# Gathered rows copied by ScalarE before TensorE weights them, one round later

## The chip, the cores and the metric

The kernel runs on one core of one Trainium2 chip. The metric is the device time of one execution in microseconds. Before the change it is 7,739.45 us, the median of three runs (7,736.22 to 7,743.75).

## The reference, cut to what matters

Four layers follow each other on a tensor of 4 images, 256 channels, 64 x 64 pixels; each adds its result to its input. The change is in layer 0, a deformable convolution. For every pixel, each of 4 groups of 64 channels and each of 9 points, an offset is computed from the image, and the padded image is read at that place between four neighbouring pixels. The four readings are weighted by the position and by a softmax mask, and the nine points are added up:

```python
return tap(x0, y0, (1 - wx) * (1 - wy)) + tap(x0 + 1, y0, wx * (1 - wy)) + tap(x0, y0 + 1, (1 - wx) * wy) + tap(x0 + 1, y0 + 1, wx * wy)
...
samp = _grid_sample(img, sg)
mr = mask.reshape(n, H * W, G, P).transpose(0, 2, 1, 3).reshape(n * G, 1, H * W, P)
dout = (samp * mr).sum(-1).reshape(n, G * GC, H * W).transpose(0, 2, 1).reshape(n, H, W, C)
dout = jnp.einsum('nhwc,oc->nhwo', dout, outproj_w) + outproj_b
```

The places depend on the data, so the readings are gathers. The rest of layer 0 (convolutions, a squeeze-and-excite and two large matrix products called the feed-forward), layer 1 (linear attention with a 5 x 5 depthwise convolution), layer 2 (a 3 x 3 convolution) and layer 3 (attention against a pooled map) are dense work.

## The kernel before, in words

Each image has a table in HBM (`tab`) in which one row holds the 2 x 2 neighbourhood of a pixel for one group: 256 values of fp32, 1 KB. `sample(n, ssum)`, lines 556 to 686, does the gathering of image n in rounds. A round is 14 pixels by 9 points, 126 of the 128 partitions, and all four groups. An image has 4,096 pixels, so it has 293 rounds in 19 blocks of up to 16; four images have 1,172 rounds.

What happens to round i, and on which engine:

- `gathered`, lines 596 to 608: GpSimd issues four indirect DMAs, one a group (line 600), each of 128 rows of 1 KB, into a tile `g` of 4 KB a partition. There are seven such tiles (`bufs=7`), so the first DMA of round i waits until TensorE has read the tile of round i - 7. The four DMAs also use eight landing semaphores in turn, so each waits until the DMA eight before it has landed.
- Still in `gathered`, line 607: TensorE multiplies the four landed pieces with a small weight matrix `wm`, 8 matmuls of 128 columns, which the trace records as 16. They add up into one half of a PSUM bank, `acc`; two rounds make a unit.
- `weigh`, line 591: VectorE makes `wm` for four rounds at once, four rounds ahead, into one of two buffers.
- `moved`, line 612: ScalarE copies the unit's sums to SBUF (`at`). `turned`, line 617: TensorE transposes them. `spread`, line 632: ScalarE puts them in their places (`dT`). `project`, `add`, `finish` (lines 640, 644, 649): a matmul, an addition and a scaling at the end of each block.

**What sets the order.** The order on TensorE, VectorE, ScalarE and GpSimd is the order in which the program issues instructions: `ordered()`, line 1217, switches the scheduler's own reordering off for these four. Each engine works through its own queue and stops at the first instruction whose semaphores are not there yet. Two things decide what stands where in the queues:

- The dictionary `later` in `sample`. Step i of the loop first runs what has been put down for step i, then issues the gathers of round i. Before the change, `moved`, `turned` and `spread` of a unit that ends in round i run at steps i + 1, i + 2 and i + 3 (the last one step later in the first rounds of a block).
- `beside`, line 1194. After each step it lets other generators advance in proportion: beside image 0 the convolutions and offsets of images 1 to 3; beside image n the feed-forward of image n - 1 during the first fifth of the rounds and its layer 1 (`linear`) after that, and beside images 2 and 3 also layers 2 and 3 of image n - 2. Their instructions stand between the steps of `sample` in the same queues. This document calls them the side work.

GpSimd's queue holds nothing but gathers while images are sampled. After the last gather, dense work of images 2 and 3 remains.

Of the kernel before, what the change touches and what calls it, by code (L numbers as in the profile page):

```python
# [9 lines left out]
F32 = mybir.dt.float32  # L10
# [7 lines left out]
P = 128  # L18
N, C, H, W = 4, 256, 64, 64
HW = H * W  # L20
KT = C // P
NB = HW // 512
NT = HW // P
G, PT = 4, 9
# [5 lines left out]
RP, WR, UR, BR = 14, 4, 2, 16  # L30
# [41 lines left out]
class Net:  # L72
# [483 lines left out]
    def sample(self, n, ssum):  # L556

        nc, sp = self.nc, self.sp
        table = self.tab[n].rearrange("g y x s c -> (g y x) (s c)")
        blocks, images, at, dp, dT, po, later = {}, {}, {}, {}, {}, {}, {}

        def halves(name):

            t = self.ps1.tile([P, 2, 256], F32, name=name, tag=name)
            return cycle([t[:, 0], t[:, 1]])

        accs, dps = halves("acc"), halves("dp")  # L570

        def load(b):
            p0, np_ = BLOCKS[b]
            whole, part = np_ // RP, np_ % RP

            nr = whole + (part > 0)
            sl = sp.tile([P, BR, G * 5], F32, name="sl")
            rows = self.s_d[n][p0 * PT:p0 * PT + nr * RS, :].rearrange("(r p) f -> p r f", p=RS)
            more = self.s_d[n][p0 * PT + RS:p0 * PT + (nr + 1) * RS, :].rearrange("(r p) f -> p r f", p=RS)
            nc.sync.dma_start(sl[0:RS, 0:nr], rows)  # L580
            nc.sync.dma_start(sl[RS:P, 0:nr], more[0:P - RS])
            rounds = [(r, RP) for r in range(whole)] + [(whole, part)] * (part > 0)
            blocks[b] = sl, rounds

        def weigh(b, r):

            sl, rounds = blocks[b]
            nu = min(WR, len(rounds) - r)
            wm = self.gp.tile([P, WR, 4 * G, OB], F32, name="wm")
            sh = [P, nu, 4 * G, OB]  # L590
            nc.vector.tensor_tensor(  # L591
                wm[:, 0:nu], self.con("own").unsqueeze(1).unsqueeze(1).to_broadcast(sh),
                sl[:, r:r + nu, G:].unsqueeze(3).to_broadcast(sh), ALU.mult)
            return wm

        def gathered(sl, wm, acc, r):
            r4, acc = r % WR, acc[:, r % UR * P:(r % UR + 1) * P]
            g = self.gp.tile([P, G, 256], F32, name="g", bufs=7)
            for i in range(G):
                nc.gpsimd.indirect_dma_start(  # L600
                    out=g[:, i, :], out_offset=None, in_=table,
                    in_offset=bass.IndirectOffsetOnAxis(ap=sl.bitcast(I32)[:, r, i:i + 1], axis=0))


            for x in range(2):
                for i in range(G):
                    nc.tensor.matmul(acc[32 * i:32 * i + 32, :], wm[:, r4, 4 * i + 2 * x:4 * i + 2 * x + 2, :],  # L607
                                     g[:, i, x * P:(x + 1) * P], start=x == 0, stop=x == 1)

        def moved(acc, nu, u):  # L610
            at[u] = sp.tile([P, UR, P], F32, name="at")
            nc.scalar.copy(at[u].rearrange("p v c -> p (v c)")[:, 0:nu * P], acc[:, 0:nu * P])  # L612

        def turned(nu, u):
            dp[u] = next(dps).rearrange("p (v g s o) -> p v g s o", v=UR, g=G, s=2)
            for v in range(nu):
                nc.tensor.transpose(dp[u][:, v].rearrange("p g s o -> p (g s o)"), at[u][:, v], self.ident)  # L617

        def spread(unit, b, u):

            if b not in dT:
                p0, np_ = BLOCKS[b]
                dT[b] = sp.tile([P, G, BP], F32, name="dT", bufs=1)
                images[b] = sp.tile([P, KT, BP], F32, name="yb")
                nc.sync.dma_start(images[b][:, :, 0:np_], self.y_d[n][:, :, p0:p0 + np_])
            full = sum(1 for _, m in unit if m == RP)
            for v0, v1, m in ((0, full, RP), (full, len(unit), unit[-1][1])):
                for s in range(2):
                    if v0 < v1:
                        hs = slice(64 * s, 64 * s + 64)  # L630
                        q0 = RP * (unit[0][0] + v0)
                        nc.scalar.copy(  # L632
                            dT[b][hs, :, q0:q0 + m * (v1 - v0)].rearrange("p g (v o) -> p g v o", o=m),
                            dp[u][hs, v0:v1, :, s, 0:m].rearrange("p v g o -> p g v o"))

        def project(b, m):
            np_ = BLOCKS[b][1]
            po[m] = self.ps("po")
            for k in range(G):
                nc.tensor.matmul(po[m][:, 0:np_], self.ow[:, k, m * P:(m + 1) * P], dT[b][:, k, 0:np_], start=k == 0, stop=k == G - 1)  # L640

        def add(b, m):
            ym = images[b][:, m, 0:BLOCKS[b][1]]
            nc.vector.tensor_tensor(ym, po[m][:, 0:BLOCKS[b][1]], ym, ALU.add)

        def finish(b, m):
            p0, np_ = BLOCKS[b]
            ym = images[b][:, m, 0:np_]
            nc.scalar.activation(ym, ym, AF.Identity, bias=self.sh[:, 4 + m:5 + m],
                                 scale=self.inv[:, 4 + m:5 + m], accum_out=ssum[:, m, b:b + 1])  # L650
            if m == KT - 1:
                nc.sync.dma_start(self.x2_d[n][:, :, p0:p0 + np_], images[b][:, :, 0:np_])

        load(0)
        order = [(b, r) for b, (_, np_) in enumerate(BLOCKS) for r in range(-(-np_ // RP))]
        wm = weigh(0, 0)
        for i, (b, r) in enumerate(order):
            for f in later.pop(i, ()):
                f()
            sl, rounds = blocks[b]  # L660
            if r % UR == 0:
                acc = next(accs)
            gathered(sl, wm, acc, r)
            if r == 0 and b + 1 < len(BLOCKS):
                load(b + 1)
            ends = r + 1 == len(rounds)
            if r % WR == 0:
                if r + WR < len(rounds):
                    nxt = weigh(b, r + WR)
                elif b + 1 < len(BLOCKS):  # L670
                    nxt = weigh(b + 1, 0)
            if r % UR == UR - 1 or ends:
                unit = rounds[r - r % UR:r + 1]
                todo = [partial(moved, acc, len(unit), i), partial(turned, len(unit), i), partial(spread, unit, b, i)]

                todo = [(i + 1 + j + (j == 2 and r < UR), f) for j, f in enumerate(todo)]
                if ends:
                    todo += [(i + 4 + m + j, partial(f, b, m)) for m in range(KT) for j, f in enumerate((project, add, finish))]
                for j, f in todo:
                    later.setdefault(j, []).append(f)  # L680
            if r % WR == WR - 1 or ends:
                wm = nxt
            yield 1
        for i in sorted(later):
            for f in later[i]:
                f()
# [656 lines left out]
```

## Time and profile before

| what | value |
|---|---|
| median of the timed runs | 7,739.45 us |
| span of the profiled execution (the page gives no other time for it) | 8,805.8 us |
| first and last start of a gather in it | 134.1 and 7,306.6 us |
| busy, TensorE / VectorE / ScalarE / GpSimd | 5,993.9 / 5,173.3 / 2,183.8 / 5,152.4 us |
| mean granted TensorE clock | 0.809 |
| gathers | 4,688 indirect DMAs, 614.77 MB, 225,024 packets |
| share of the DMA engines' time, gathers / other copies | 24.3% / 16.4% |

How to read it. The profiled execution is 1,066.4 us longer than the median of the timed runs, so durations of single instructions can be taken from it, but not all of its waiting. A GpSimd gather counts as busy while GpSimd makes its descriptors; the data lands later. Idle time ahead of an instruction is put down to the work whose semaphore ended it ("releaser"); "remote" stands for a release that the profile can't put down to a recorded end, and "issue" for a gap in which nothing was waited for. The lines of the page that matter are shown with the prediction.

### The profile page before, as it was taken

How to read it: one execution, taken by the hardware profiler on the slowest of the kernel's cores; microseconds unless marked ns; L12 is line 12 of the kernel's file. 1: busy time of each engine (PE TensorE's matmuls, PEld its weight loads, DVE VectorE, ACT ScalarE, POOL GpSimd, SP SyncE). 2: the span in 40 equal slices, each digit the busy share in tenths (PEclk: the TensorE clock that was granted, in tenths of full speed). 3: DMA queues.
4: the chain of work that ended last, by engine and by line, in shares of the span. 5: the costliest groups of instructions: out<-in, count | busy, mean ns of one | idle time of the engine just before them, and what ended most of it. 6: DMA issues, size and time to landing. Idle time of an engine off the chain costs nothing. (4 is left out here: it accounts for less than half of the span.)

```text
span 8805.8 us, 95736 instructions
## 1 busy us (share of the span) xinstructions
PE 5993.9 (68%) x36532; PEld 3575.6 (41%) x36532; DVE 5173.3 (59%) x6409; ACT 2183.8 (25%) x4899; POOL 5152.4 (59%) x4950
## 2 busy tenths in 40 slices
PE   4454554448744446688876677888766778986899
PEld 2222222224323322244544443345544433664477
DVE  5444443443466667424777776227777772599834
ACT  1111111112211112122223222222222222465524
POOL 2666666566666666666666656666666661376410
PEclk7676766669866667799988888898878888998999
DMA  6454454444433334444443344444434343220131
GB/s 172 127 155 124 141 154 118 125 145 145 153 105 105 110 105 129 127 130 138 134 135 110 112 121 136 142 134 132 136 115 117 114 118 99 69 74 29 48 98 53
DMA packets 759050, 1042.27 MB, mean 118 GB/s; under 512 B 362432, under 2 KB 472128, under 8 KB 757056
## 3 DMA queue, kind: packets, MB, share of 16 engines
q0 software_dynamic: 225024, 614.77, 24.3%
q1 hardware_dynamic: 533568, 421.39, 16.4%
q8 instruction: 289, 4.73, 0.2%
q14 instruction: 169, 1.38, 0.0%
HBM read 867.08 MB, written 168.69 MB: 118 GB/s over the span
## 5 line engine op out<-in xcount | busy, mean ns | idle before, releaser
L600 POOL DMA_INDIRECT g<-tab,sl x4688 | 4618.5, 985 | 2687.8 <-issue 1224.2
L178 DVE SCALAR_TENSOR_TENSOR agg<-pad,vec,agg 128x1024 f32<-128x1024 f32 x2280 | 2933.5, 1287 | 61.9
L607 PE MATMUL acc<-g,wm 128*32 128x128 f32 x18752 | 1034.8, 333 | 1907.8 <-ACT at L612 1273.7
L607 PEld LDWEIGHTS acc<-g,wm 128*32 128x32 f32 x18752 | 566.8, 128 | 2411.7 <-ACT at L612 1446.1
L1048 PE MATMUL ps<-xd,w 128*128 128x256 f32 x3072 | 752.7, 396 | 51.3 <-issue 37.8
L591 DVE TENSOR_TENSOR wm<-con,sl 128x1024 f32<-128x1024 f32 (+1 forms) x296 | 357.7, 1209 | 711.9 <-remote 533.5
L1048 PEld LDWEIGHTS ps<-xd,w 128*128 128x128 f32 x3072 | 595.1, 199 | 175.0 <-issue 86.0
L632 ACT COPY dT<-dp 64x112 f32<-64x112 f32 x1176 | 285.9, 243 | 1043.7 <-remote 544.3
L742 PE MATMUL ps<-x2f,f 128*128 128x512 f32 x1024 | 499.2, 636 | 19.1 <-issue 7.7
L817 PE MATMUL ps<-xr,qw 128*128 128x512 f32 x768 | 472.0, 746 | 22.1 <-issue 11.1
L727 DVE SCALAR_TENSOR_TENSOR hm<-ps,vec,lk 128x512 f32<-128x512 f32 x256 | 190.8, 750 | 492.9 <-ACT lk L744 405.5
L752 PE MATMUL ps<-hm,f 128*128 128x512 f32 x1024 | 467.1, 605 | 0.9 <-DVE hm L727 0.9
L612 ACT COPY at<-acc 128x256 f32<-128x256 f32 (+1 forms) x588 | 218.3, 371 | 986.3 <-remote 753.2
L999 POOL TENSOR_TENSOR xd<-xp 128x640 f32<-128x640 f32 x64 | 79.4, 1268 | 492.6 <-ACT xp L1011 298.3
L640 PE MATMUL po<-dT,ow 128*128 128x224 f32 (+1 forms) x1216 | 326.1, 419 | 45.4 <-issue 19.3
L617 PE MATMUL dp<-ident,at 128*128 128x128 f32 x1172 | 284.1, 330 | 106.6 <-ACT dT L632 61.0
L865 ACT COPY kt<-pt 128x512 f32<-128x512 f32 x256 | 149.4, 584 | 829.3 <-remote 403.8
L744 ACT ACTIVATE lk<-ps,low 128x512 f32<-128x512 f32 x256 | 174.0, 687 | 666.0 <-PE ps L742 512.1
L1147 PE MATMUL s<-ph,th 128*128 128x512 f32 x512 | 290.2, 672 | 62.5 <-ACT kt L865 15.9
L640 PEld LDWEIGHTS po<-dT,ow 128*128 128x128 f32 x1216 | 265.5, 233 | 113.8 <-issue 68.9
L1167 PEld LDWEIGHTS ps<-gt,pT 128*128 128x128 f32 x2048 | 276.0, 213 | 70.8 <-issue 46.1
L194 POOL TENSOR_TENSOR ak<-ak,m 128x1024 f32<-128x1024 f32 x96 | 228.1, 2376 | 130.6 <-ACT m L193 126.7
(243 smaller groups left out, 8022.0 us busy)
## 6 DMA issues: line engine op xcount, KB each, us to landing
g<-tab,sl POOLq DMA_INDIRECT x4688
x<-x SPq DMA_DIRECT2D x128, 512.0 KB
xr<-x SPq DMA_DIRECT2D x96, 512.0 KB
tab<-xo SPq DMA_DIRECT2D x192, 128.0 KB
x<-in_x SPq DMA_DIRECT2D x32, 512.0 KB
y<-yc SPq DMA_DIRECT2D x32, 512.0 KB
x2f<-x SPq DMA_DIRECT2D x32, 512.0 KB
xyf<-x SPq DMA_DIRECT2D x32, 512.0 KB
```

What stands on the lines that cost most here:

```text
L178: nc.vector.scalar_tensor_tensor(to, s, wt, acc, ALU.mult, ALU.add)
L591: nc.vector.tensor_tensor(wm[:, 0:nu], self.con("own").unsqueeze(1).unsqueeze(1).to_broadcast(sh), sl[:, r:r + nu, G:].unsqueeze(3).to_bro ...
L600: nc.gpsimd.indirect_dma_start(out=g[:, i, :], out_offset=None, in_=table, in_offset=bass.IndirectOffsetOnAxis(ap=sl.bitcast(I32)[:, r, i: ...
L607: nc.tensor.matmul(acc[32 * i:32 * i + 32, :], wm[:, r4, 4 * i + 2 * x:4 * i + 2 * x + 2, :], g[:, i, x * P:(x + 1) * P], start=x == 0, st ...
L617: nc.tensor.transpose(dp[u][:, v].rearrange("p g s o -> p (g s o)"), at[u][:, v], self.ident)
L632: nc.scalar.copy(dT[b][hs, :, q0:q0 + m * (v1 - v0)].rearrange("p g (v o) -> p g v o", o=m), dp[u][hs, v0:v1, :, s, 0:m].rearrange("p v g ...
L640: nc.tensor.matmul(po[m][:, 0:np_], self.ow[:, k, m * P:(m + 1) * P], dT[b][:, k, 0:np_], start=k == 0, stop=k == G - 1)
L742: nc.tensor.matmul(ps, f1[:, k, m * P:(m + 1) * P], x2[:, k], start=k == 0, stop=k == KT - 1)
L752: nc.tensor.matmul(ps, f2[:, k, m * P:(m + 1) * P], hm[:, k], start=k == 0, stop=k == 4 * KT - 1)
L817: nc.tensor.matmul(ps, qw[:, k, m * P:(m + 1) * P], x[:, k], start=k == 0, stop=k == KT - 1)
L1048: nc.tensor.matmul(ps[:, e], w[:, k, t, 2 * half + e, m * P:(m + 1) * P], v[:, 2 * half + e, k, t:t + 8], start=i % 6 == 0, stop=i % 6 == 5)
L1147: nc.tensor.matmul(s[i], tv[:, 4 * b + j], ph[:, i * 512:(i + 1) * 512], start=True, stop=True)
```

## The change

Round i is split over three steps. At step i GpSimd issues the gathers, now into four tiles `g`. At step i + 1 ScalarE copies the landed tile, 128 partitions by 1,024 values, to one of three tiles `gc`. At step i + 2 TensorE weights the copy. A tile `g` is thus free when ScalarE has copied it, and a tile `gc` when TensorE has read it. The memory is the same: 4 + 3 tiles in place of 7. What follows the weighting moves by two steps (`moved`, `turned`, `spread`), `project`, `add` and `finish` by three, and `weigh` is issued at steps 2, 6, 10 and 14 of a block for the same rounds as before, so still four steps ahead of its use.

```diff
-        def gathered(sl, wm, acc, r):
-            r4, acc = r % WR, acc[:, r % UR * P:(r % UR + 1) * P]
-            g = self.gp.tile([P, G, 256], F32, name="g", bufs=7)
+        def gathered(sl, r):
+            g = self.gp.tile([P, G, 256], F32, name="g", bufs=4)
             for i in range(G):
                 nc.gpsimd.indirect_dma_start(
                     out=g[:, i, :], out_offset=None, in_=table,
                     in_offset=bass.IndirectOffsetOnAxis(ap=sl.bitcast(I32)[:, r, i:i + 1], axis=0))
-
-
+            return g
+
+        def copied(g, i):
+            held[i] = self.gp.tile([P, G, 256], F32, name="gc", bufs=3)
+            nc.scalar.copy(held[i], g)
+
+        def weighted(wm, acc, r, i):
+            r4, acc, g = r % WR, acc[:, r % UR * P:(r % UR + 1) * P], held.pop(i)
             for x in range(2):
                 for i in range(G):
                     nc.tensor.matmul(acc[32 * i:32 * i + 32, :], wm[:, r4, 4 * i + 2 * x:4 * i + 2 * x + 2, :],
...
-            gathered(sl, wm, acc, r)
+            g = gathered(sl, r)
+            for j, f in ((1, partial(copied, g, i)), (2, partial(weighted, wm, acc, r, i))):
+                later.setdefault(i + j, []).append(f)
...
-            if r % WR == 0:
-                if r + WR < len(rounds):
-                    nxt = weigh(b, r + WR)
+            if r % WR == 2:
+                if r + 2 < len(rounds):
+                    nxt = weigh(b, r + 2)
                 elif b + 1 < len(BLOCKS):
                     nxt = weigh(b + 1, 0)
...
-                todo = [(i + 1 + j + (j == 2 and r < UR), f) for j, f in enumerate(todo)]
+                todo = [(i + 3 + j + (j == 2 and r < UR) * (7 - 5), f) for j, f in enumerate(todo)]
                 if ends:
-                    todo += [(i + 4 + m + j, partial(f, b, m)) for m in range(KT) for j, f in enumerate((project, add, finish))]
+                    todo += [(i + 7 + m + j, partial(f, b, m)) for m in range(KT) for j, f in enumerate((project, add, finish))]
```

In the built program the number and the order of GpSimd's gathers are the same as before; the first gather of each round now waits for ScalarE's semaphore where it waited for TensorE's. ScalarE's queue has 1,172 more copies. Within a step the program issues `moved` ahead of the copy, so that in ScalarE's queue each second copy stands right behind an `at` copy, and the side work of the step stands behind both.

More of the change, by code (lines that the diff above doesn't have):

```diff
@@ L562, in sample @@
         table = self.tab[n].rearrange("g y x s c -> (g y x) (s c)")
-        blocks, images, at, dp, dT, po, later = {}, {}, {}, {}, {}, {}, {}
+        blocks, images, at, dp, dT, po, held, later = {}, {}, {}, {}, {}, {}, {}, {}
         def halves(name):
```

## The prediction

> **What bounds the kernel now.** I read the groups of the page first, then who waited on GpSimd, then its timeline, then the busy times by stretch.
>
> ```profile
> L600 POOL DMA_INDIRECT g<-tab,sl x4688 | 4618.5, 985 | 2687.8 <-issue 1224.2
> L607 PE MATMUL acc<-g,wm 128*32 128x128 f32 x18752 | 1034.8, 333 | 1907.8 <-ACT at L612 1273.7
> L612 ACT COPY at<-acc 128x256 f32<-128x256 f32 (+1 forms) x588 | 218.3, 371 | 986.3 <-remote 753.2
> L865 ACT COPY kt<-pt 128x512 f32<-128x512 f32 x256 | 149.4, 584 | 829.3 <-remote 403.8
> ```
>
> ```profile
> POOL g L600 <- issue: 1224.2, 4007, 0.7
> POOL g L600 <- remote: 624.7, 307, 6.0
> POOL g L600 <- PE acc L607: 494.3, 201, 23.2
> ```
>
> ```profile
> 1009.60 0.95 POOL L600 DMA_INDIRECT g<-tab,sl  x1 [0.30 <-issue]
> 1010.85 0.95 POOL L600 DMA_INDIRECT g<-tab,sl  x1 [0.30 <-issue]
> 1013.81 0.94 POOL L600 DMA_INDIRECT g<-tab,sl  x1 [2.02 <-remote]
> ```
>
> A gather takes GpSimd 0.95 us and 0.30 us to the next: 1.25 us, 5.0 us a round. 4,688 x 1.25 = 5,860 us. From the first gather at 134.1 to the end of the last at 7,307.5 us are 7,173 us, so 1,313 us are longer gathers and stops. The stops stand at the first gather of a round, the one that waits for a free tile: GpSimd has used up its seven tiles and TensorE has not read the oldest. "Remote" is the same wait: at 1,013.81 TensorE's recorded matmuls had ended earlier than the release.
>
> ```profile
> 3669.00:4050.00 381.00, 315.54 (x1654) 148.61 (x1644) 93.76 (x132) 82.33 (x193) 240.40 (x249) 0.92 0.46 135
> 4050.00:5487.00 1437.00, 1049.87 (x7011) 669.40 (x7010) 1053.45 (x1241) 371.64 (x916) 903.92 (x924) 0.85 0.44 127
> ```
>
> Columns: stretch, length, busy PE, PEld, DVE, ACT, POOL, clock, DMA. The first stretch is the feed-forward beside image 2: 249 gathers are 62 rounds, 315.5 / 62 = 5.1 us of TensorE a round against GpSimd's 5.0. In the second, 231 rounds, VectorE needs 1,053.5 / 231 = 4.6 us a round. GpSimd bounds, but TensorE, then VectorE, are within 10%. ScalarE is the idle one: 371.6 of 1,437.
>
> The profiled execution is 1,066.4 us longer than the median. If a gather costs the same without the profiler and the rest keeps its length, a timed run has room for only 1,313 - 1,066 = 247 us of stops. GpSimd is then nearly the whole bound of the gathering stretch.
>
> **What the Trainium skill says.** "DMA: Bandwidth & Descriptors", section on the anatomy of one SWDGE DMA: "DMA engines do not wait on semaphores"; the wait is on the issuing sequencer. So one full ring holds all gathers behind it, as the timeline shows. The page gives some 2.0 us from issue to completion; here 225,024 packets / 4,688 are 48 a gather, and in order of time the 48th ends 1.4 to 2.5 us after its issue: it agrees. "GPSIMD Engine Reference", section "When to use GPSIMD": GpSimd's cores generate the descriptors, so the 0.95 us are not shortened by how the data is used later. "ScalarE: Activation LUTs", section "What ACT_TABLE_LOAD costs": 186 ns + 0.833 ns an element with immediate operands. The trace has 372 ns (median) for 256 columns and 584 for 512, a slope of 0.83: it agrees.
>
> **The change, part by part.**
>
> *The copies.* 1,172 copies of 1,024 columns. From the trace, 584 + 2 x 212 = 1,008 ns, read from PSUM; from the page an estimate of 1,039. I take 1.04 us: 1,172 x 1.04 = 1,219 us more ScalarE, 2,184 -> 3,403. Per image ScalarE gets 305 us on top of 248, 340, 454 and 454 (busy by image): at most 759 of 1,821 us. It does not become the bound by load. What it can do is delay the ScalarE link of a chain: `lk` before VectorE's `hm`, `kt`, `pr`, `at`. Such an instruction finds a copy running with chance 1.04 / 6.1 = 17%, and then waits 0.52 us: 0.09 us each. Images 2 and 3 have 1,108 ScalarE instructions in 293 rounds, 3.8 a round; if two of them are waited for, 0.18 us a round. That is paid only where side work is behind GpSimd; I take 40% of the 879 rounds of images 1 to 3: 0.18 x 352 = 65 us. Bounds: 0, if PSUM and tile buffers cover it; 0.34 x 879 = 300 us if all 3.8 count everywhere. The copy also waits, for its landing and for a `gc` tile, and the side work of the step stands behind it. Landing comes 2.5 us after GpSimd's round, the copy a step later, so this wait costs nothing while GpSimd is a round ahead.
>
> *The shorter ring.* The memory stays seven tiles, but they no longer give one distance. Before, GpSimd stops when TensorE has not finished round i - 7: six rounds, 30.0 us, less 2.5 of landing and some 1.0 of matmuls, about 26 us that TensorE may be held. Now it stops when ScalarE has not copied round i - 4: three rounds, 15.0 - 2.5 - 1.04 = 11.5 us that ScalarE may be held. And ScalarE's queue is held by all others: each second copy stands behind `at`, which waits for TensorE. In the gathering stretch ScalarE idled over 11.5 us 63 times; the excess over 11.5 is 81 us in 32 waits with a named releaser (VectorE's `agg`, TensorE's `ps`) and 130 us in 31 "remote" ones, 53 of it in one wait at the start of sampling that comes before any ring is full. Where GpSimd was stopped anyway, nothing is lost. I take three quarters of the named: 60 us. Bounds: 0 and 81 + 77 = 158.
>
> *The later weighting.* TensorE no longer stops for a landing. TensorE waited for landings 9 times, 30.7 us, 21.1 of them at the first round of all, which stays. Gain 0 to 10 us; I take 0, since such a stop comes when GpSimd is the late one. `wm` is still made four steps ahead of its use and waits for the same TensorE step, so VectorE's waits do not move. `acc` is reused at the same distance. No DMA is added or moved past another on GpSimd's queue; on SP's the loads of `sl` and the stores of blocks keep their steps within three.
>
> *The end.* One more copy after the last landing: 1 us. At the ends of images 0 to 2 GpSimd goes on with the next image and covers it.
>
> Sum: 65 + 60 + 0 + 1 = +126 us. Against the profiled execution's own time that is 8,805.8 + 126 = 8,932 us of span; the page gives no time around the span. The work added is the same in a timed run, so I put the same sum on the median: 7,739.45 + 126 = 7,865 us (+1.6%). What is late next, once GpSimd has stopped for a copy, is TensorE or VectorE as before; they get no shorter.
>
> **The rivals.**
>
> *Hidden, 7,739 us.* ScalarE is idle for 60% of every image even with the copies, and the total of seven tiles is kept. For it: the side work's matmuls have three PSUM tiles in turn (`mm`), so a ScalarE delay of 1 us is mostly buffered. Against it: ScalarE's long waits, which the ring must now absorb.
>
> *Faster, 7,640 us.* A tile is freed by ScalarE as soon as it landed, not by TensorE after everything ahead of it in its queue. The place is GpSimd's wait at line 600. Its price: the stops named after TensorE, 494.3 - 201 x 0.30 = 434 us, of which half, the copies that do not stand behind an `at`, could go: 217 us in the profile; a timed run has room for 247 us of stops in all, so about 100 there. It decides where TensorE is late and ScalarE is not, by more than one step: `at` waits for TensorE every second step, so ScalarE can't run away from it. That speaks against it.
>
> *ScalarE sets the pace of side work, 8,105 us.* If each copy stands in a chain TensorE - ScalarE - VectorE, then 879 rounds x 1.04 us x 40% = 366 us. For it: TensorE's greatest wait is already for ScalarE's `at` (1,273.7 us). Against it: those waits end with TensorE's own completion, and ScalarE itself is idle in them.
>
> **How the numbers follow.** Forecast 0.62, its own range 7,800 (the copies cost nothing, +61) to 7,970 (half of both upper bounds, (300 + 158) / 2 = 229). Hidden 0.12. Faster 0.12. ScalarE pacing 0.14. A difference of 0.2%, 15 us, is about what a measurement of this kernel tells from no change. Slower: 0.62 + 0.14 = 0.76; same 0.12; faster 0.12. The range of 7,690 to 8,110 starts halfway between the faster and the hidden case and ends just past the pacing case: it leaves out half of each of the two outer cases, 0.06 + 0.07, and with the forecast's own tails about 0.17.
>
> **What would show it.** Right: GpSimd's waits at the first gather named after ScalarE's `gc` copy and longer in sum than the 1,119 us of before; gathers still 0.95 + 0.30 us; copies of about 1.04 us, ScalarE busy near 3,400 us; TensorE's weighting waiting for almost nothing but `gc`. The ring is the larger cost if the stops grow where ScalarE waits long; the copies, if TensorE's and VectorE's waits for ScalarE's side work grow instead. Wrong: stops well below 1,119 us, or a gather with another duration; also if the sampling ends at the same time and the difference lies in the dense work after it, which the change doesn't touch.

## The result, and the profile after

The changed kernel takes 7,831.5 us (median of 4 runs, 7,825.3 to 7,834.7) against 7,741.6 us for the kernel before (4 runs): a ratio of 1.0111, 95% interval 1.0099 to 1.0123. It is slower by 90 us, where the forecast had 126.

One thing is needed to read the numbers. The profile of before shown ahead of the prediction seems to come from a chip of a second sort. On two such chips the unchanged kernel took 8,820 and 8,755 us in timed runs (experiments 4 and 6), at granted clocks of 0.80 to 0.81; that profile has 8,805.8 us and 0.809. On the other chips the kernel takes 7,740 us, at 0.84 to 0.85. If so, the 1,066 us between that profile and the timed runs come from the chip, and not from the profiler. A second profile of before, on a chip of the first sort, has a span of 7,730.1 us, close to its timed runs, and no "remote" at GpSimd's gathers; it is what the profile after (span 7,823.5 us) is compared with. I call it "before, again".

Groups of before, again, with all releasers the view gives (busy us, mean ns of one | idle before it):

```profile
L600 POOL DMA_INDIRECT g<-tab,sl x4688 | 4593.2, 980 | 1651.7 <-issue 1311.9 <-DMA sl<-sd 135.6 <-PE acc L607 112.2
L607 PE MATMUL acc<-g,wm 128*32 128x128 f32 x18752 | 1328.3, 319 | 1101.5 <-DMA g<-tab,sl 575.5 <-ACT at L612 517.4 <-issue 3.1
L612 ACT COPY at<-acc 128x256 f32<-128x256 f32 (+1 forms) x588 | 218.3, 371 | 625.8 <-PE acc L607 604.4 <-issue 12.8 <-ACT dT L632 0.3
```

The same groups after:

```profile
L599 POOL DMA_INDIRECT g<-tab,sl x4688 | 4584.6, 978 | 1761.1 <-issue 1304.6 <-ACT gc L606 236.0 <-DMA sl<-sd 132.4
L606 ACT COPY gc<-g 128x1024 f32<-128x1024 f32 x1172 | 1218.9, 1045 | 1706.9 <-DMA g<-tab,sl 1706.2 <-ACT ot L922 0.2
L612 PE MATMUL acc<-gc,wm 128*32 128x128 f32 x18752 | 933.7, 328 | 1521.4 <-ACT at L617 1254.4 <-ACT gc L606 266.5
L617 ACT COPY at<-acc 128x256 f32<-128x256 f32 (+1 forms) x588 | 218.2, 371 | 41.0 <-PE acc L612 18.6 <-PE ps L759 10.3
```

A gather costs GpSimd what it did (978 and 980 ns, and the same gaps named "issue"). The waits for landings, 575.5 us, have gone from TensorE and are now ScalarE's, 1,706.2 us: whoever reads the tile first waits for GpSimd, and since GpSimd bounds, that need not cost time (experiment 2). These landings make up 1,706.2 of the 1,706.9 us that ScalarE idled ahead of its copies, so the three tiles `gc` never held it up. What changed on the engine that bounds stands in the first line of each fence: 112.2 us of waits for TensorE became 236.0 us of waits for ScalarE's copy. GpSimd's waits in order of size (us in total, times, longest) show it again, first before, again, then after:

```profile
POOL g L600 <- issue: 1311.9, 4306, 0.6
POOL g L600 <- PE acc L607: 112.2, 88, 7.0
```

```profile
POOL g L599 <- issue: 1304.6, 4282, 0.6
POOL g L599 <- ACT gc L606: 236.0, 129, 21.5
```

From the first gather to the end of the last are 6,109.3 us in before, again, and 6,213.3 after, 104 us more; what follows the last gather is 7 us shorter. So the loss lies in the gathering stretch. There I count **stops**: the gap ahead of a round's first gather where it is over 0.35 us, less the usual 0.30, and without the first of all. They sum to 87 us in before, again, and 197 after. The 110 us more cover the whole loss.

The stretches of image 2, feed-forward first and then layer 1 with layers 2 and 3 of image 0, in before, again (length, busy PE, PEld, DVE, ACT, POOL with the number of instructions, clock, DMA share, GB/s):

```profile
3168.00:3480.00 312.00, 276.81 (x1495) 132.27 (x1494) 85.95 (x119) 73.80 (x170) 235.13 (x244) 0.96 0.53 159
3480.00:4703.00 1223.00, 981.57 (x7148) 636.48 (x7147) 1055.02 (x1253) 380.86 (x938) 910.18 (x930) 0.90 0.51 150
```

and after:

```profile
3201.30:3523.00 321.70, 287.25 (x1546) 136.70 (x1547) 88.07 (x122) 131.79 (x236) 229.30 (x237) 0.96 0.51 151
3523.00:4774.00 1251.00, 995.41 (x7151) 649.66 (x7150) 1054.44 (x1250) 603.99 (x1166) 916.09 (x937) 0.89 0.51 148
```

In the long stretch VectorE does the same work (1,055 and 1,054 us) and GpSimd too, ScalarE has 223 us more and is still busy for less than half of it. The stretch is 28 us longer, of which some 9 are the seven gathers more that fall into it (937 against 930). No engine got full; GpSimd was let go later.

### The profile page after: what moved, and what is told of

Read it like the earlier page. It is cut to its first block, busy times and chain, and to the rows that moved or that the text cites. A ratio compares the mean times of both kernels' runs of the same rounds, so it can differ in the third digit from the quotient of the medians.

```text
span 7823.5 us, 98450 instructions
## 1 busy us (share of the span) xinstructions
PE 5714.5 (73%) x36532; PEld 3477.0 (44%) x36532; DVE 5157.9 (66%) x6409; ACT 3319.8 (42%) x6071; POOL 5118.5 (65%) x4950
## 5 line engine op out<-in xcount | busy, mean ns | idle before, releaser
L612 PE MATMUL acc<-gc,wm 128*32 128x128 f32 x18752 | 933.7, 328 | 1521.4 <-ACT at L617 1254.4
L606 ACT COPY gc<-g 128x1024 f32<-128x1024 f32 x1172 | 1218.9, 1045 | 1706.9 <-DMA g<-tab,sl 1706.2
L612 PEld LDWEIGHTS acc<-gc,wm 128*32 128x32 f32 x18752 | 531.1, 126 | 1973.0 <-ACT at L617 1486.6
L1055 PE MATMUL ps<-xd,w 128*128 128x256 f32 x3072 | 715.1, 386 | 21.4 <-ACT kt L872 15.0
L645 PE MATMUL po<-dT,ow 128*128 128x224 f32 (+1 forms) x1216 | 302.8, 401 | 21.4 <-DVE yb L649 8.8
L1174 PE MATMUL ps<-gt,pT 128*128 128x128 f32 x2048 | 296.9, 306 | 6.7 <-ACT pT L1170 6.6
L1161 ACT ACTIVATE pe<-s,mx 128x512 f32<-128x512 f32 x256 | 173.6, 683 | 302.0 <-DVE mx L1156 302.0
L749 PEld LDWEIGHTS ps<-x2f,f 128*128 128x128 f32 x1024 | 191.4, 195 | 234.1 <-issue 217.0
L194 POOL TENSOR_TENSOR av<-av,m 128x1024 f32<-128x1024 f32 x96 | 226.7, 2362 | 99.8 <-ACT m L193 95.4
```

Source lines behind the costliest of these rows:

```text
L194: nc.gpsimd.tensor_tensor(acc, acc, m, ALU.add)
L606: nc.scalar.copy(held[i], g)
L749: nc.tensor.matmul(ps, f1[:, k, m * P:(m + 1) * P], x2[:, k], start=k == 0, stop=k == KT - 1)
L1055: nc.tensor.matmul(ps[:, e], w[:, k, t, 2 * half + e, m * P:(m + 1) * P], v[:, 2 * half + e, k, t:t + 8], start=i % 6 == 0, stop=i % 6 == 5)
L1174: nc.tensor.matmul(ps[:, 0:P], pT[:, m], gt[:, m], start=m == 0, stop=m == 7)
```

## Where one stop comes from

The longest stop after, in GpSimd's timeline (start, us; in brackets the idle time before it and what ended it):

```profile
1366.51 0.94 POOL L599 DMA_INDIRECT g<-tab,sl  x1 [0.30 <-issue]
1367.76 0.95 POOL L599 DMA_INDIRECT g<-tab,sl  x1 [0.30 <-issue]
1390.16 1.28 POOL L599 DMA_INDIRECT g<-tab,sl  x1 [21.45 <-ACT gc L606]
```

and ScalarE's timeline over the same time:

```profile
1351.26 1.04 ACT L606 COPY gc<-g 128x1024 f32<-128x1024 f32 x1 [4.76 <-DMA g<-tab,sl]
...
1357.29 1.02 ACT L482 ACTIVATE t<-agg 128x1024 f32<-128x1024 f32 x1 [4.32 <-DVE agg L178]
1371.59 1.02 ACT L482 ACTIVATE t<-agg 128x1024 f32<-128x1024 f32 x1 [13.27 <-DVE agg L178]
1387.71 0.44 ACT L537 ACTIVATE ml<-ml 128x288 f32<-128x288 f32 x1 [15.10 <-DVE ml L536]
...
1388.84 1.99 ACT L606 COPY gc<-g 128x1024 f32<-128x1024 f32 x2
```

Between the copy that ended at 1,352.3 and the one that started at 1,388.84 ScalarE copied nothing for 36.5 us. The offsets of a later image stood in its queue, and three of their instructions in a row waited for VectorE: 4.3, 13.3 and 15.1 us. Four tiles let GpSimd issue three rounds past the one that ScalarE owes, about 15.0 us; 36.5 - 15.0 = 21.5 us is the length of the stop. In before, again, the corresponding stop is 7.0 us, although ScalarE is held longer there:

```profile
1394.81 1.04 POOL L600 DMA_INDIRECT g<-tab,sl  x1 [6.96 <-PE acc L607]
```

```profile
1362.41 1.02 ACT L482 ACTIVATE t<-agg 128x1024 f32<-128x1024 f32 x1 [15.34 <-DVE agg L178]
1376.70 1.02 ACT L482 ACTIVATE t<-agg 128x1024 f32<-128x1024 f32 x1 [13.27 <-DVE agg L178]
1392.14 0.44 ACT L537 ACTIVATE ml<-ml 128x288 f32<-128x288 f32 x1 [14.42 <-DVE ml L536]
```

There TensorE, which frees the tiles, waits for ScalarE's `at` behind these three, but seven tiles stand between it and GpSimd.

A wait of ScalarE is only the beginning of a stop. Summed over all 72 stops of after (218.6 us, the usual 0.30 us of each included), ScalarE waited for other engines for 66 us. For 58 us it was copying gathered tiles, for 75 us it did other work, and 19 us lie between the end of a copy and the gather that it lets go. So the stop lasts until ScalarE has worked off what piled up ahead of the copy that is owed.

## Experiments

Each is compared with the kernel before, run beside it on the same chip. The table has the kernels run on chips of the first sort: the time, its ratio, then from the profile the sum of the stops and the time from an image's first gather to the next one's (for image 3, to the end of its last gather).

| kernel | median us | ratio (95%) | stops | image 0 | 1 | 2 | 3 |
|---|---|---|---|---|---|---|---|
| before, again | 7,738.9 | 1.0006 (0.9997 to 1.0014) | 87 | 1,518.2 | 1,514.7 | 1,535.1 | 1,541.3 |
| lag_only | 7,745.4 | 1.0010 (1.0004 to 1.0017) | 108 | 1,526.1 | 1,519.2 | 1,547.0 | 1,544.7 |
| copies_only | 7,788.3 | 1.0064 (1.0050 to 1.0078) | 144 | 1,524.9 | 1,515.2 | 1,565.1 | 1,572.1 |
| ring4 | 7,833.0 | 1.0130 (1.0112 to 1.0147) | 192 | 1,553.7 | 1,528.5 | 1,571.7 | 1,562.1 |
| after | 7,831.5 | 1.0111 (1.0099 to 1.0123) | 197 | 1,549.2 | 1,518.4 | 1,572.6 | 1,573.1 |
| thin4_b | 7,807.1 | 1.0083 (1.0069 to 1.0096) | 167 | 1,548.8 | 1,521.7 | 1,556.0 | 1,556.2 |
| thin7_b | 7,750.7 | 1.0007 (1.0001 to 1.0014) | 100 | 1,517.5 | 1,521.0 | 1,542.2 | 1,545.9 |

My theory at the start of this part: GpSimd bounds, and it pays for the shorter ring and for the copies' time on ScalarE in about equal parts. The rivals: the ring alone; the copies alone; the later weighting.

**1. The kernel before, unchanged** (before_again), to have a profile to compare with.

> The kernel before, unchanged, for a second profile. The profile of the changed kernel has a span of 7,823.5 us, within 8 us of its median, and its GpSimd is rarely stopped; the first profile of before was 1,066 us longer than its median. If that first profile was disturbed, this one has a span near 7,740 us, next to no waits named remote, and stops of GpSimd at the first gather of a round of about 100 us in place of 1,119. If the profiler always stretches this kernel, the span is again near 8,800 us.

Measured 7,738.9 us and the profile used above. The waits named "remote" are absent, so they belong to the first profile's chip and not to the kernel.

**2. The later weighting alone** (lag_only): TensorE weights the gathered tile itself two steps later; seven tiles, no copies.

```diff
+        def copied(g, i):
+            held[i] = g
...
-            gathered(sl, wm, acc, r)
+            g = gathered(sl, r)
+            for j, f in ((1, partial(copied, g, i)), (2, partial(weighted, wm, acc, r, i))):
+                later.setdefault(i + j, []).append(f)
```

(with the other steps of the queue moved as in the change)

> One part alone: TensorE weights two rounds after the gather, as in the changed kernel, but reads the gathered tile itself; seven tiles g, no copies. Ring theory and copy theory: the lag costs nothing of its own; GpSimd now stops when TensorE's step is five rounds behind it where it was seven, so 7,740 to 7,760 us. Rival, that the lag itself costs (later chain at block ends, weights made at another step): 7,790 to 7,830 us. A gain is possible if TensorE's stops for landings mattered: 7,700 us.

Measured +0.1%, some 7 us, as both theories had it. It gains nothing, although TensorE in before, again, waited 575.5 us for landings. Its waits in lag_only:

```profile
PE acc L611 <- DMA g<-tab,sl: 597.1, 706, 21.2
PE acc L611 <- ACT at L616: 526.4, 308, 12.1
```

They are still there: TensorE reaches the weighting early whatever its place in the queue, because GpSimd is the late one.

**3. The copies alone, and the shorter ring alone.** copies_only is the kernel before in which ScalarE also copies 1,024 columns of a constant a round, in three pieces, to a tile that nobody reads; by the profile they take 1.43 us a round (two of 512 ns, one of 405) in place of 1.045, and they wait for no gather. ring4 is the kernel before with four gather tiles.

```diff
+            spare, flat = self.gp.tile([P, 384], F32, name="gc", bufs=1), self.ow.rearrange("p g c -> p (g c)")
+            for a, b in ((0, 384), (384, 768), (768, 1024)):
+                nc.scalar.copy(spare[:, 0:b - a], flat[:, a:b])
```

```diff
-            g = self.gp.tile([P, G, 256], F32, name="g", bufs=7)
+            g = self.gp.tile([P, G, 256], F32, name="g", bufs=4)
```

> The other cost alone: the kernel before with seven tiles, and in each round ScalarE also copies 1,024 constant columns (in three pieces, about 1.2 us) to a spare tile that nothing reads and that wait for nothing but each other. Copy theory: 7,800 to 7,850 us, with VectorE's and TensorE's waits for ScalarE grown. Ring theory: within 25 us of before, since ScalarE has the idle time.

> One cost alone: the kernel before with four gather tiles in place of seven, TensorE reading them in the same step. GpSimd stops when TensorE has not finished the round four before. Ring theory: slower by as much as the change or more, 7,820 to 7,950 us, with stops of GpSimd growing by that amount. Copy theory: the ring has slack to spare, within 15 us of before.

Measured +0.64% (50 us) for the copies and +1.30% (101 us) for the ring. The ring's 7,833 us are where the ring theory had them; the copies' 7,788 us lie above what the ring theory allowed and below what the copy theory had. Each alone is a cost, and with lag_only they make 2.04%, nearly twice the 1.11% of the change: they do not add up. The place differs too. copies_only loses 30 us in each of images 2 and 3 in the profiled execution, which was the slowest of its five. Most of it lies in rounds 240 to 269 (201.2 us against 172.4 in image 2, against 178.7 in image 3), where layers 1 to 3 run beside the gathers. ring4 loses in all four images, 36 us of it in image 0, where one stop alone is 23.3 us (7.0 before):

```profile
POOL g L600 <- PE acc L607: 230.1, 127, 23.3
```

What each part costs inside the changed kernel was still open. The next pair asks that.

**4. The changed kernel with small copies** (thin4), and with seven gather tiles on top (thin7). Small copies free the memory for it. Both leave out most of the gathered values, so what they add up is not the convolution.

```diff
-            held[i] = self.gp.tile([P, G, 256], F32, name="gc", bufs=3)
-            nc.scalar.copy(held[i], g)
+            held[i] = self.gp.tile([P, G, 32], F32, name="gc", bufs=3)
+            nc.scalar.copy(held[i], g[:, :, 0:32])
...
-                                     g[:, i, x * P:(x + 1) * P], start=x == 0, stop=x == 1)
+                                     g.rearrange("p g c -> p (g c)"), start=x == 0, stop=x == 1)
```

> The changed kernel (four gather tiles, three of the copy, weighting two steps later), but ScalarE copies only 32 of each round's 4x256 gathered columns per slot, and all eight matmuls read these 128 columns. It leaves out the other columns, so that its output is not the convolution; gathers, waits and order stay. ScalarE loses some 0.77 us a round (1,045 ns down to about 270 ns, 900 us in sum). If the shorter ring is the cost (a stall that ScalarE or GpSimd inherits from other work costs GpSimd time once four rounds are out), the time stays within 7,800 to 7,830 us, and GpSimd's gathers still wait for the copy some 150 to 240 us. If the time of the copies themselves is the cost, it falls to 7,745 to 7,770. I expect the first, with a part of the second: 7,800.

> As the one before, but with seven gather tiles in place of four (the small copies leave room). Copies, their order and the later weighting stay, so only the length of the ring differs between the two. If the ring is the cost, 7,735 to 7,755 us, as the kernel before, and waits of gathers for the copy under 100 us. If what costs is that GpSimd waits for a queue with more in it (ScalarE, behind at) whatever the ring, it stays over 7,780.

Both ran on a chip on which the kernel before took 8,820.1 us: 9,529.8 us (ratio 1.0785, 1.0758 to 1.0812) and 9,522.3 us (1.0799, 1.0779 to 1.0819). Neither theory had such numbers. On this chip four tiles or seven make no difference with small copies, so the ring is not the cost there. Experiment 6 has more of it.

**5. The same two kernels, on a chip of the first sort.**

> The kernel with copies of 32 columns a slot and four gather tiles once more (it leaves out the other columns), because the call before ran on a chip on which the kernel before takes 8,820 us. On a chip where the kernel before takes 7,740 us: ring theory 7,800 to 7,830 us, copy theory 7,745 to 7,770; I expect 7,800. On a chip such as the last one: 9,530 again.

> The kernel with copies of 32 columns a slot and seven gather tiles once more. On a chip where the kernel before takes 7,740 us: ring theory 7,735 to 7,755 us; if a stop comes whatever the ring, over 7,780. On a chip such as the last one: 9,520 again.

7,807.1 and 7,750.7 us, both as the ring theory had it. Their groups of the copy, and GpSimd's wait for it, thin4_b first:

```profile
L606 ACT COPY gc<-g 128x128 f32<-128x128 f32 x1172 | 343.8, 298 | 2251.6 <-DMA g<-tab,sl 2249.6 <-issue 1.4
```

```profile
POOL g L599 <- ACT gc L606: 195.2, 98, 18.6
```

and thin7_b:

```profile
POOL g L599 <- ACT gc L606: 126.6, 87, 8.9
```

This splits the change in three, in ratios, each to the kernel before that ran beside it. The time of the copies, 1,045 down to 298 ns: 1.0111 - 1.0083 = 0.28%, 22 us. The ring, four tiles to seven: 1.0083 - 1.0007 = 0.76%, 59 us. What is left, the later weighting and the small copies: 0.07%, 5 us. The ring's part rests on two kernels that differ in the number of tiles alone; it is measured with small copies, and with full ones it may differ. The copies' part is barely resolved by the times (one interval starts at 1.0099, the other ends at 1.0096), and the changed kernel and thin4_b were not run side by side. The profiles place it: after loses to thin4_b 16.6 and 16.9 us in images 2 and 3 and nothing in images 0 and 1. The ring's 56 us in the profiles are 31 in image 0, 1 in image 1, and 14 and 10 in images 2 and 3. The stop at 1,390 us is 21.5 us after, 18.6 in thin4_b and 4.7 in thin7_b, whose ScalarE is held for as long:

```profile
1384.03 0.95 POOL L599 DMA_INDIRECT g<-tab,sl  x1 [0.30 <-issue]
1389.72 0.95 POOL L599 DMA_INDIRECT g<-tab,sl  x1 [4.74 <-ACT gc L606]
```

How the copies' own time acts is seen at one stop of image 3, the same round in both; after and then thin4_b:

```profile
6034.63 0.95 POOL L599 DMA_INDIRECT g<-tab,sl  x1 [0.30 <-issue]
6044.01 0.94 POOL L599 DMA_INDIRECT g<-tab,sl  x1 [8.44 <-ACT gc L606]
```

```profile
6014.58 0.95 POOL L599 DMA_INDIRECT g<-tab,sl  x1 [0.30 <-issue]
6021.37 0.95 POOL L599 DMA_INDIRECT g<-tab,sl  x1 [5.85 <-ACT gc L606]
```

Short copies don't remove the stop, they make it 2.6 us shorter. In both kernels ScalarE had just waited for a matmul (`pad<-ps`, 6.12 and 5.24 us), and the copy that frees the tile stands behind that. Of the 2.6 us, 0.75 are the copy itself (1.04 against 0.29). The other 1.8 us are wait: GpSimd ran out of free tiles earlier, so 4.8 us of ScalarE's wait fall into the stop in after, and 2.9 in thin4_b. Over all stops the difference is plain. ScalarE spends 58 us of them in copies of gathered tiles in after, and 12 us in thin4_b.

**6. Order and split of the tiles.** copy_first puts the copy ahead of `moved` and `spread` in its step; g5c2 has five gather tiles and two of the copy.

```diff
-                later.setdefault(i + j, []).append(f)
+                later.setdefault(i + j, []).insert(0 if j == 1 else len(later.get(i + j, ())), f)
```

```diff
-            g = self.gp.tile([P, G, 256], F32, name="g", bufs=4)
+            g = self.gp.tile([P, G, 256], F32, name="g", bufs=5)
...
-            held[i] = self.gp.tile([P, G, 256], F32, name="gc", bufs=3)
+            held[i] = self.gp.tile([P, G, 256], F32, name="gc", bufs=2)
```

> The changed kernel with ScalarE's copy issued ahead of at and dT in its step instead of behind them. My prediction counted the place behind at as a part of the cost of the shorter ring (ScalarE held for TensorE's sums): if that holds, at most 30 us fall away, 7,800 to 7,831. If the stops come from other work that holds ScalarE (activations of the second image's layers, which wait for VectorE), the order inside the step changes nothing: 7,825 to 7,840. I expect the latter.

> The changed kernel with five gather tiles and two of the copy, seven in all as before. If the number of gather tiles is the cost, one more gives GpSimd one round (5 us) more before a stop: some 30 us less, 7,790 to 7,810. If the copies' time on ScalarE is the cost, 7,825 to 7,840; if the copies' own tiles hold ScalarE up (TensorE has not weighted the last but one), slower than 7,840. I expect the first.

> The changed kernel with ScalarE's copy ahead of at and dT in its step, once more, hoped for on a chip where the kernel before takes 7,740 us. Smaller copies brought 24 us of the 90 (7,807 us), seven gather tiles with them 56 more (7,751). If standing behind at is what turns a late copy into a stop, 7,800 to 7,820 us; if other work holds ScalarE, 7,825 to 7,840; slower than that if at and dT, now late by a copy, hold TensorE's sums. I expect the second. On a chip such as the one of the first try, 9,700.

> The changed kernel with five gather tiles and two of the copy, once more. The ring was worth 56 us between four tiles and seven with small copies: if each tile takes its part of it, the first of them most, 7,795 to 7,815 us; if the second copy tile less is felt (TensorE has not yet weighted the copy before), 7,831 or more. I expect the first. On a chip such as the one of the first try, 9,530.

Both tries fell on chips of the second sort (kernel before: 8,820.1 and 8,754.5 us). copy_first: 9,705.9 and 9,644.4 us, ratios 1.1003 (1.0981 to 1.1024) and 1.1016 (1.0993 to 1.1039). g5c2: 9,535.0 and 9,457.0 us, 1.0816 (1.0792 to 1.0841) and 1.0797 (1.0769 to 1.0824). g5c2 with its full copies thus comes out near thin4 and thin7, and copy_first is slower than g5c2 by some 2% (9,705.9 / 9,535.0 = 1.018; 9,644.4 / 9,457.0 = 1.020). The two differ in the split of the tiles as well as in the order, and the changed kernel itself was not run on such a chip. That the order is what costs the 2% is likely, since neither the ring nor the size of the copies made a difference there, but not shown. My question was about chips of the first sort and is not answered for them.

What differs on such a chip is that TensorE's results come late by the profile. In thin7 there, GpSimd's waits, ScalarE's waits and ScalarE's timeline with TensorE's:

```profile
POOL g L599 <- ACT gc L606: 2005.3, 478, 36.0
```

```profile
ACT at L617 <- remote: 856.1, 152, 36.5
ACT dT L637 <- remote: 696.3, 63, 18.6
```

```profile
4516.87 0.78 ACT L830 ACTIVATE v<-ps,g_add,vec 128x512 f32<-128x512 f32 x1 [10.13 <-remote]
...
4519.18 0.30 ACT L606 COPY gc<-g 128x128 f32<-128x128 f32 x1
```

```profile
4510.99 1.98 PE L824 MATMUL ps<-xr,qw 128*128 128x512 f32 x4
```

The matmuls for `v` are recorded as over at 4,513.0 us; `v` could start at 4,516.9, and the next copy stands behind it. Of the `at` copies that ScalarE was held for, the median start is about 4.3 us after the recorded end of their matmuls (thin7) and 2.9 us in the first profile of before, against 0.1 us in before, again. Waits put down to VectorE or ScalarE end within 0.02 us of the recorded end in nine of ten cases in all of these profiles, so TensorE alone is late. The ends of matmuls are modelled in the profile; whether the matmuls last longer than recorded or are reported late, it doesn't tell. Copies (298 ns) and gathers (974 ns) last what they do elsewhere. In 95% of the rounds of images 1 to 3 of thin7 there TensorE's recorded weighting stands seven or more rounds behind GpSimd; in the first profile of before it is six behind, all that seven tiles allow, in 81%, and in before, again, in 23%. So on these chips the ring is nearly always full, GpSimd follows the others, and a longer ring doesn't help. The new link from ScalarE back to TensorE may then be paid once a round, on top of a late result; 8% would be some 0.6 us a round. No run separates this.

## Why the prediction was right, step by step

- **GpSimd bounds, and a timed run has room for 247 us of stops.** Right that GpSimd bounds; the 247 us are stops and longer gathers together. Before, again, has a stretch of 6,109 us against 4,688 x 1.25 = 5,860: 249 us, of which 87 are stops. The reason given, that the profiler adds time, was wrong, and the sum came out because gathers and the part after them last nearly the same on both sorts of chip. TensorE's 5.1 us a round in the feed-forward was the other chip's: here 276.8 us over 61 rounds are 4.5. VectorE's 4.6 in the next stretch stands (1,055.0 / 232.5 = 4.5). The 1.4 to 2.5 us to a landing count from the end of GpSimd's own part of a gather; from its start they are 2.35 to 3.5 in the first profile (80% of the gathers).
- **The shorter ring: 60 us, bounds 0 to 158.** Right in mechanism and size: 59 us between thin4_b and thin7_b. The place was partly right: waits for `agg` and for a matmul's `ps` begin the stops looked at. The count carries over to the other sort of chip (excess over 11.5 us in before, again: 80.5 us in 27 waits). But three quarters was a guess, and single waits are not the measure: the longest stop comes from three waits in a row with no copy between, 36.5 us in all, and most of the stops' time is work that has piled up. That 60 met 59 so closely is luck in part.
- **Each second copy stands behind `at`.** Not shown to cost anything. ScalarE idled 41.0 us ahead of `at` in the whole of after, 18.6 of them for TensorE's sums, and the `at` copies take 7.8 us of the stops. On chips of the second sort the kernel with the copy ahead of it was 2% slower than g5c2.
- **The copies: 65 us, bounds 0 to 300.** The duration was right (1,045 ns measured, 1,040 taken; by the rate in "ScalarE: Activation LUTs" of the Trainium skill, section "What ACT_TABLE_LOAD costs", the estimate was 1,039). The cost was mis-sized: 22 us for 747 ns of it, 31 us if the rest goes in proportion (22 x 1,045 / 747). That makes up the difference between 126 and 90 (0.18 x 352 are 63 and not 65, which matters little). The factor "40% of the 879 rounds of images 1 to 3" fails: in the profiles image 1 pays nothing, and in copies_only most of it falls in some 30 rounds each of images 2 and 3.

  The way was wrong too. The forecast let the copies delay ScalarE's link in the chains of the side work. The chain it named first, `lk` before VectorE's `hm`, waits no longer than before (before, again, then after):

```profile
DVE hm L727 <- ACT lk L744: 410.1, 230, 17.4
DVE hm L734 <- ACT lk L751: 406.5, 221, 18.3
```

  Another, `lk` before `yc`, does (before, again, after, thin4_b, thin7_b):

```profile
DVE yc L374 <- ACT lk L373: 109.6, 34, 9.3
DVE yc L374 <- ACT lk L373: 319.5, 53, 17.8
DVE yc L374 <- ACT lk L373: 320.1, 52, 18.4
DVE yc L374 <- ACT lk L373: 286.4, 50, 18.5
```

  But it waits as long with small copies, and nearly as long in thin7_b, which loses 0.07%. In copies_only, whose copies wait for no landing, it is 144.6 us. So these waits come from ScalarE's wait for the landings and not from the length of the copies, and they cost next to nothing, as the forecast said of that wait. What shrinks with the copies is their own time inside GpSimd's stops, 58 us against 12.
- **The later weighting: 0.** Right within 7 us. The reason given was wrong in part: on this sort of chip TensorE waited for landings not 9 times but 693 times, 575.5 us, and taking these waits away gained nothing.
- **The end: +1 us.** The part after the last gather is 7 us shorter; nothing of the loss lies there, as the text had it.
- **What would show it.** The copies' duration, ScalarE's load (3,319.8 us against "near 3,400"), the gathers' 0.95 + 0.30 us and the name of the new wait came as said. Two tests were set wrongly. "Longer in sum than the 1,119 us of before" took its number from a chip where GpSimd waits for late results; the sum is 236.0 against 112.2. For the same reason "stops well below 1,119 us", named as a sign of being wrong, came true without the forecast being wrong. And TensorE's weighting waits mostly for `at` (1,254.4 us), not for `gc` (266.5).
- **The rivals.** Hidden fails by 1.11%; with seven tiles and small copies it would nearly be true (thin7_b, +0.07%). Faster: its mechanism may be there, since at four gather tiles the kernel that frees them by a short copy is faster than the one in which TensorE frees them (thin4_b 1.0083, ring4 1.0130), though these two also differ in the later weighting. The three tiles given to the copies cost more. ScalarE pacing fails: copies shorter by 747 of 1,045 ns bring 22 us, where 366 were forecast for the whole.

Open remains what the order of copy and `at` is worth on a chip of the first sort, and what makes TensorE's results late on the second.

## What to carry over

When a buffer pool is split in two stages, count for the producer only the tiles of the first stage, and compare their time with the longest stretch in which the freeing engine does not reach its next release; add up its waits and its work across the instructions of side work that stand between two releases. Giving the release to an engine that is idle 60% of the time helps little if that engine's queue holds work that waits for others. An engine's waits that grow with a change say little on their own: in thin7_b VectorE's grew by some 180 us at one instruction, and the kernel lost 0.07%. Waits of a consumer for its producer are no gain to be had when the producer is the bound.

## What the runs showed of the hardware that was not expected

The same program takes 7,740 us on one chip (experiments 1 to 3 and 5) and 8,820 and 8,755 us on two others, with gathers and copies of the same length; the mean granted TensorE clock differs little (0.849 and 0.809), but TensorE's results reach ScalarE about 2.9 us (median of the held `at` copies) after the recorded end instead of 0.1. The loss of a change depends on it: thin7 costs 0.07% on the first sort and 8.0% on the second. Before a profile is used for counting stops, its span should be held against the timed runs; where they differ by a tenth, as 8,805.8 and 7,739 us did here, its stops are those of another chip.
